# One more group gathered from the raw rows in a graph-network kernel, with its rows turned inside the group loop

## The chip, the cores and the metric

The kernel runs on one core of a Trainium2 chip. The metric is device time in microseconds, the median of several runs; lower is better. The engines are named as in the profile: PE (TensorE), DVE (VectorE), ACT (ScalarE), POOL (GpSimd) and SP (SyncE). SP, ACT and POOL also issue DMA transfers.

## The reference

There are 6250 nodes with 128 features and 100000 edges, sorted by destination, with 4 features each. All is float32.

```python
msg_in = concatenate([x[src], x[dst], edge_features], axis=1)
h = silu(msg_in @ mW1 + mb1)
messages = h @ mW2 + mb2
aggregated = segment_sum(messages, dst, num_segments=N)
u = silu(concatenate([x, aggregated], axis=1) @ uW1 + ub1)
updated = u @ uW2 + ub2
y = layer_norm(x + updated, ln_g, ln_b)
out = layernorm(x + y)
```

## The kernel before

**The algebra.** The first matrix `mW1` is split by its rows into a part for the source node, one for the destination node and one for the edge's features. Two tables of node rows are computed first: `tab_a = x @ (source part)` and `tab_b = x @ (destination part) + mb1`. Both are written to device memory. An edge's hidden row is then the row of `tab_a` at its source, plus a product which supplies the destination's and the edge features' share. Sums over destinations are made before the second matrix, so that `mW2` and the upper part of `uW1` can be merged into one matrix, `w2u` (`fuse_weights`).

**Groups.** Edges are worked in 98 groups of 1024, each of 8 tiles of 128 edges (the last has 6). For group g, `fetch(g)` (L273) has POOL issue one indirect DMA per tile, each of which gathers 128 rows of 512 bytes into the tile `ga`. There are 6 such buffers, in turn, so that group 6 takes the buffer of group 0 and so on. `products(g)` (L627) multiplies on PE a matrix `st` (which edge belongs to which of 96 nearby destinations, made by `node_matrix` on DVE, and the edge's features) with `mv` (96 rows of `tab_b` from the group's first destination, loaded by `load(g)` from SP, and the features' weights). `hidden(g)` (L640) adds the gathered rows on DVE and applies SiLU on ACT. `edge_matrix(g)` makes the one-hot `oh` on DVE, `by_nodes(g)` sums on PE the hidden rows by destination, and `add(g)` puts the sums into the accumulator `acc` on DVE.

**The first groups.** `tab_a` isn't written yet when the first gathers can start. So groups below `RAW`, here 5, gather rows of `x` itself. Those rows have to be multiplied by `w1`, and for that they are first turned by PE transposes: `turn_rows(g)` (L357) transposes the eight tiles of a group into a PSUM tile `wide` and has DVE copy them back over `rows[g]`. `products(g)` then adds one product of the turned rows per tile (L634), and `hidden(g)` has no addition on DVE. In the profile a float32 product counts as two MATMUL instructions, a transpose as one. The tables are computed in the loop of L367 beside all this; `turn_rows(0)` to `turn_rows(4)` are issued in it or just behind it, `products(0)` and `products(1)` follow at L685, before the loop of groups.

**The order of work** is written out by hand: the tile framework does not reorder the engines' instructions, each engine takes them in the order of the program. It still adds the waits that data need: a gather into a buffer that was used before waits for its last reader. Beside these, `fetch(g, a, b)` makes the first gather of a group wait for the PE instruction a and its fifth for b. The loop of groups (L688) runs at each g: the loads of group g + 4, `hidden(g)`, `products(g + 2)`, `node_matrix(g + 3)`, `edge_matrix(g + 1)`, `add(g - 2)`, `by_nodes(g)`, a `fetch`, and one step of each generator in `running`. Group 6 is fetched before the loop (L687), 7 at g = 0, 8 at g = 1, one group at every odd g up to 11, and from g = 12 on group g + 2.

**Side work as generators.** `destination_checks` (L230) tests whether all destinations of a group lie within 96 of its first, and whether finished nodes are really finished; if not, a general path runs at the end. It is begun at g = 2. `fuse_weights` (L450) is begun at g = 8. `node_batch` computes the output of four tiles of nodes at a time, first at g = 10. All three take their PSUM tile from `node_y` (L422), a pool with one buffer.

Of the kernel before, what the change touches and what calls it, by code (L numbers as in the profile page):

```python
# [24 lines left out]
def kernel(  # L25
# [40 lines left out]
    nc = tc.nc  # L66
# [5 lines left out]
    G = 8  # L72
# [6 lines left out]
    RB = 14  # L79
    CLOSE = 14  # L80
    LEAD = 4
    RAW = 5
    MADE = 3
    NQ = 4
    NM = 5
    BT = 4
# [28 lines left out]
    def wide():  # L115
        return tables_ps.tile([P, G, P], F32, name="wide")
# [51 lines left out]
    ident = consts.tile([P, P], F32, name="ident")  # L168
# [58 lines left out]
        nc.vector.tensor_copy(base_f, row)  # L227
        nc.vector.tensor_copy(base_i, row)

    def destination_checks(pm):  # L230

        nc.tensor.matmul(pm[:, 0, :NG], ones[0:1, :], base_f, start=True, stop=True)
        yield
        yield
        nc.vector.tensor_scalar(base_p, pm[:, 0, :NG], p_col, None, op0=OP.add)

        far = work.tile([P, 2], F32, name="far", bufs=1)
        nc.vector.tensor_reduce(far[:, 0:1], rel, AX.XY, OP.max)
        nc.vector.tensor_reduce(far[:, 1:2], rel, AX.XY, OP.min)
        mid = (W - 1) / 2  # L240
        nc.vector.tensor_scalar(far, far, -mid, None, op0=OP.add)
        nc.vector.tensor_mul(far, far, far)
        nc.vector.tensor_reduce(far[:, 0:1], far, AX.X, OP.max)
        farthest = work.tile([1, 1], F32, name="farthest", bufs=1)
        yield
        nc.tensor.transpose(pm[0:1, 1, :], far[:, 0:1], ident)
        yield
        yield
        nc.vector.tensor_reduce(farthest, pm[0:1, 1, :], AX.X, OP.max)
        bad = work.tile([1, 2], F32, name="bad", bufs=1)  # L250
        nc.vector.tensor_scalar(bad[:, 0:1], farthest, mid * mid, None, op0=OP.is_gt)

        below = work.tile([1, NG], F32, name="below", bufs=1)
        nc.vector.memset(below, 0.0)
        for i0, n, g in batches[:-1]:
            nc.vector.memset(below[:, g:], float((i0 + n) * P))
        nc.vector.tensor_sub(below, below, base_f)
        nc.vector.tensor_reduce(bad[:, 1:2], below, AX.X, OP.max)
        nc.vector.scalar_tensor_tensor(
            bad_i, bad[:, 1:2], 0.0, bad[:, 0:1], op0=OP.is_gt, op1=OP.max  # L260
        )
# [6 lines left out]
    rows, bases, near = {}, {}, {}  # L268

    def tiles_of(g):  # L270
        return min(G, -(-(E - g * GE) // P))

    def fetch(g, *after):  # L273

        rows[g] = gath.tile([P, G, H], F32, name="ga")
        for i in range(tiles_of(g)):
            ins = nc.gpsimd.indirect_dma_start(  # L277
                out=rows[g][:, i, :],
                out_offset=None,
                in_=x if g < RAW else tab_a[:, :],  # L280
                in_offset=bass.IndirectOffsetOnAxis(
                    ap=src_i[:, g, i : i + 1] if g else src_0[:, i : i + 1], axis=0
                ),
            )
            part, at = divmod(i * len(after), G)
            if after and at == 0 and after[part]:
                tc.add_manual_dep(
                    ins.ins,
                    after[part].ins.name,
                    mybir.DependencyInfo(  # L290
                        mybir.DependencyClass.Sync, mybir.DependencyReason.DATA
                    ),
                    reason="TensorE keeps up with the gathers",
                )
# [41 lines left out]
    def turn_x(i0, n):  # L336
        pt = wide()
        for i in range(n):
            ins = nc.tensor.transpose(pt[:, i, :], x_sb[:, i0 + i, :], ident)
        nc.scalar.copy(xT[:, i0 * P : (i0 + n) * P], pt[:, :n, :].rearrange("p i f -> p (i f)"))  # L340
        return ins
# [15 lines left out]
    def turn_rows(g):  # L357

        px = wide()
        for i in range(G):  # L360
            ins = nc.tensor.transpose(px[:, i, :], rows[g][:, i, :], ident)
        nc.vector.tensor_copy(rows[g], px)
        return ins

    turn_x(*parts[0])
    fetch(1)
    for k, (i0, n) in enumerate(parts):  # L367
# [5 lines left out]
        for j0, m in groups(n, G // 2):  # L373
            pm = wide().rearrange("p (i s) f -> p i s f", s=2)
# [24 lines left out]
        if k == 4:  # L399
# [1 line left out]
            destinations(0)  # L401
            load_bases(0)
            turn_rows(1)
    fetch(RAW, None, turn_rows(2))
    for g in range(3, RAW):
        turn_rows(g)
    if E < NG * GE:
        pad = tpool.tile([ED, NG * GE - E], F32, name="pad")
# [13 lines left out]
    def node_y():  # L422
        return node_ps.tile([P, BT, H], F32, name="y")
# [26 lines left out]
    def fuse_weights():  # L450
        pm = node_y()
        nc.tensor.transpose(pm[:, 0, :], raw_w["w2"], ident)
        yield
        w2T = work.tile([P, P], F32, name="w2T", bufs=1)
        nc.scalar.copy(w2T, pm[:, 0, :])
        yield
        nc.tensor.matmul(pm[:, 1, :], w2T, raw_w["u1a"], start=True, stop=True)
        nc.tensor.matmul(pm[0:1, 2, :], raw_w["mb2"], raw_w["u1a"], start=True, stop=True)
        yield
        nc.scalar.copy(w2u, pm[:, 1, :])  # L460
        nc.vector.memset(mb2u, 0.0)
        for k in range(DQ):
            nc.scalar.copy(mb2u[32 * k : 32 * k + 1], pm[0:1, 2, :])
# [150 lines left out]
    def edge_matrix(g):  # L614

        oh = work.tile([P, G, W], F32, name="oh", bufs=3)
        nc.vector.tensor_tensor(  # L617
            oh,
            w_row[:, None, :].to_broadcast([P, G, W]),
            rel[:, g, :, None].to_broadcast([P, G, W]),  # L620
            op=OP.is_equal,
        )
        return oh
# [3 lines left out]
    def products(g):  # L627
        pre = rows_ps()
        st = stbuf[g % NST].rearrange("k (i c) -> k i c", i=G)
        for i in range(tiles_of(g)):  # L630
            ins = nc.tensor.matmul(pre[:, i, :], st[:, i, :], mv[g % NM], start=True, stop=g >= RAW)  # L631
            begun.setdefault(g, ins)
            if g < RAW:
                ins = nc.tensor.matmul(  # L634
# [5 lines left out]
    def hidden(g):  # L640
        h = hbuf[g % NH]
        ga = rows.pop(g)
        n = tiles_of(g)
        s = pre.pop(g)
        if g >= RAW:
            ps = s
            s = work.tile([P, G, H], F32, name="s")
            nc.vector.tensor_add(s[:, :n], ga[:, :n], ps[:, :n])  # L648
        nc.scalar.activation(h[:, :n], s[:, :n], AF.Silu)  # L649
        return h  # L650
# [14 lines left out]
    def by_nodes(g, h, oh):  # L665

        pt = degrees(g)
        sums(g, pt, h, oh, 0, tiles_of(g))
        return pt
# [14 lines left out]
    oh, h, pt, running = {0: edge_matrix(0)}, {}, {}, []  # L684
# [3 lines left out]
    for g in range(NG):  # L688
        if g == 1:
            load_weights()  # L690
        if g == 2:
            running.append(destination_checks(node_y()))
        if g == 8:
            running.append(fuse_weights())
        for c in range(1, NC):
            if g == max(1, c * EC // GE - 10):
                attributes(c)
            if g == max(1, c * EC // GE - 10) + 1:
                attribute_rows(c)
        if g + LEAD < NG:  # L700
            load(g + LEAD)
        last = g >= NG - 1
        if not last:
            h[g] = hidden(g)
        if g + 2 < NG:
            pre[g + 2] = products(g + 2)
        if g + MADE < NG:
            node_matrix(g + MADE)
        if g + 1 < NG:
            oh[g + 1] = edge_matrix(g + 1)  # L710
        if g - 2 in pt:
            add(g - 2, pt.pop(g - 2))
        if last:
            break
        pt[g] = by_nodes(g, h.pop(g), oh.pop(g))
        if CLOSE <= g + 2 < NG:
            fetch(g + 2, begun[g + 2], summing[g])
        elif g == 0:
            fetch(7, ended[1], begun[2])
        elif g == 1:  # L720
            fetch(8, begun[3], summing[1])
        elif g % 2:
            fetch(g // 2 + 8, ended[g + 1], begun[g + 2] if g == CLOSE - 3 else ended[g + 2])
        if g >= NG - 3:
            add(g - 1, pt.pop(g - 1))
        for i0, n, first in batches[:-1]:
            if g == (first if first >= NG - 3 else first + 1):
                running.append(node_batch(i0, n, *node_tiles(nodes, node_y)))
        for _ in range(0 if g == NG - 2 else 4 if g == NG - 3 else 2 if g >= NG - 6 else 1):
            advance(running)  # L730
        if g == NG - 3:
            final = node_batch(
                *batches[-1][:2],
                nodes,

                lambda name, p=P: gath.tile([P, G, H], F32, name="ga")[:p, :BT],
                lambda: rows_ps()[:, :BT],
                final=True,
            )
            next(final)  # L740
        if g == NG - 2:
            next(final)

    g = NG - 1
# [25 lines left out]
    running = [before, final]  # L770
# [159 lines left out]
```

## Time and profile before

| what | value |
|---|---|
| median of 3 runs | 1169.08 us (1167.98 to 1169.18) |
| profiled execution | 1007.52 us |
| its span, first to last instruction | 1005.4 us |
| mean granted clock of PE | 0.739 |
| busy: PE, DVE, ACT, POOL | 682.9, 487.0, 238.9, 740.0 us |
| gathers by POOL from `tab_a` | 742, mean 944 ns |
| gathers by POOL from `x` | 32 for groups 1 to 4, 8 for group 0 |
| DMA | 89.01 MB, mean 89 GB/s |

The profile is of one execution; times in it count from its first instruction. In a line of a timeline the columns are start, duration, engine, line of the kernel, operation, tile written from tiles read, shapes and count; in brackets is the idle time of the engine before it and what ended it. A wait of one engine on several others is put down to the last of them. Busy POOL time is the time in which it prepares gathers; their data move later.

### The profile page before, as it was taken

The page shows a single profiled execution, that of the slowest core. Times are in us where ns is not written, and L with a number is a line of the kernel's source. Part 1 is how long each engine was busy: PE and PEld are TensorE (multiplying, and loading weights), DVE is VectorE, ACT ScalarE, POOL GpSimd, SP SyncE. Part 2 cuts the span into 40 slices and gives each one's busy share as a digit, 9 for nine tenths or more (in the row PEclk, how much of TensorE's full clock was granted, in tenths as well). Part 3 has the DMA queues.
Part 4 walks back from the last instruction along what each step waited for, and adds up shares of the span by engine and source line. Part 5 has one row for each costly group of instructions (what it writes and reads, how often), then busy time and mean ns, then how long its engine had stood idle before and what let it go on. Part 6 is the DMA issues. An engine that isn't in the chain of part 4 may idle for free. (4 is left out here: it accounts for less than half of the span.)

```text
span 1005.4 us, 11309 instructions
## 1 busy us (share of the span) xinstructions
PE 682.9 (68%) x3645; PEld 627.6 (62%) x3645; DVE 487.0 (48%) x1018; ACT 238.9 (24%) x295; POOL 740.0 (74%) x790
## 2 busy tenths in 40 slices
PE   5869766577676567757676756767757666766854
PEld 4759756567666566756665755766656666565752
DVE  5667625444544543643554453544453454264455
ACT  2312212220321131231222122122023113122233
POOL 7767777777777777777777777777777777777771
PEclk9979977777767677667667667667767775867776
DMA  9954332232323322333233224232332332322221
GB/s 229 266 159 115 98 76 58 75 93 77 85 75 83 85 76 57 86 83 97 54 96 87 68 63 113 60 93 65 88 84 75 83 75 76 83 59 76 66 76 29
DMA packets 70076, 89.01 MB, mean 89 GB/s; under 512 B 20703, under 2 KB 51694, under 8 KB 70010
## 3 DMA queue, kind: packets, MB, share of 16 engines
q0 software_dynamic: 25024, 51.30, 20.7%
q1 hardware_dynamic: 40408, 35.03, 12.4%
q10 hardware_dynamic: 4578, 1.89, 0.9%
q8 instruction: 31, 0.51, 0.2%
q14 instruction: 35, 0.29, 0.1%
HBM read 76.78 MB, written 11.38 MB: 88 GB/s over the span
## 5 line engine op out<-in xcount | busy, mean ns | idle before, releaser
L277 POOL DMA_INDIRECT ga<-tab_a,src_i x742 | 700.7, 944 | 231.1 <-issue 210.0
L631 PE MATMUL pre<-mv,st 100*128 100x128 f32 x1564 | 328.6, 390 | 282.1 <-DVE s L648 235.6
L631 PEld LDWEIGHTS pre<-mv,st 100*128 100x128 f32 x1564 | 300.5, 293 | 304.4 <-DVE s L648 255.5
L648 DVE TENSOR_TENSOR s<-ga,pre 128x1024 f32<-128x1024 f32 x92 | 112.3, 1221 | 460.1 <-DMA ga<-tab_a,src_i 459.5
L660 PE MATMUL pt<-oh,h 128*128 128x96 f32 x1564 | 254.0, 332 | 7.2 <-DVE deg L678 3.9
L660 PEld LDWEIGHTS pt<-oh,h 128*128 128x128 f32 x1564 | 252.9, 253 | 9.4 <-ACT acc_b L500 3.3
L649 ACT ACTIVATE h<-s 128x1024 f32<-128x1024 f32 x92 | 97.2, 1057 | 649.1 <-DVE s L648 649.1
L604 DVE TENSOR_SCALAR_CACHE_REDUCE st<-near,p_next 96x1024 f32<-96x1024 uint8 x98 | 124.2, 1269 | 2.2 <-issue 1.4
L617 DVE TENSOR_TENSOR oh<-w_row,rel 128x768 f32<-128x768 f32 x98 | 93.0, 949 | 11.5 <-PE pt L660 11.5
L277 POOL DMA_INDIRECT ga<-in_x_dram,src_i x32 | 30.3, 948 | 9.8 <-issue 8.8
L649 ACT ACT_TABLE_LOAD x23 | 29.5, 1283 | 26.0 <-DMA raw_mb<-in_L_gnn_mb_dram 19.6
L489 ACT ACT_TABLE_LOAD x24 | 30.8, 1283 | 7.9 <-DVE mv L484 7.5
L530 PEld LDWEIGHTS y<-u,uT 128*128 128x128 f32 x94 | 22.5, 323 | 8.9 <-issue 8.9
L530 PE MATMUL y<-u,uT 128*128 128x128 f32 x94 | 25.2, 415 | 0.0
L678 DVE TENSOR_TENSOR deg<-deg,pt 1x96 f32 x98 | 24.4, 249 | 1.0
L673 DVE TENSOR_TENSOR acc<-acc,pt 128x96 f32 x98 | 23.6, 241 | 0.1
L377 PE MATMUL wide<-w,xT 128*128 128x256 f32 x98 | 23.1, 391 | 0.2 <-DVE rel L200 0.2
L377 PEld LDWEIGHTS wide<-w,xT 128*128 128x128 f32 x98 | 18.9, 198 | 2.9 <-DVE rel L200 0.4
L484 DVE BATCH_NORM_AGGREGATE mv<-st 128x2 f32<-128x6 f32 x98 | 17.8, 182 | 3.4
L568 ACT ACTIVATE z<-z,shift,r 128x128 f32<-128x128 f32 x47 | 19.2, 479 | 0.3 <-DVE shift L562 0.3
L545 DVE SCALAR_TENSOR_TENSOR z<-y,r,xs 128x128 f32<-128x128 f32 x47 | 16.5, 351 | 1.7
L542 DVE SCALAR_TENSOR_TENSOR y<-y,mv,g_b 128x128 f32<-128x128 f32 x47 | 16.5, 351 | 1.3
(118 smaller groups left out, 327.5 us busy)
## 6 DMA issues: line engine op xcount, KB each, us to landing
ga<-tab_a,src_i POOLq DMA_INDIRECT x742, 2.6
near<-near_d SPq DMA_DIRECT2D x24, 384.0 KB
mv<-tab_b SPq DMA_DIRECT2D x98, 48.0 KB
tab_a<-t SPq DMA_DIRECT2D x6, 512.0 KB
tab_b<-x_sb SPq DMA_DIRECT2D x6, 512.0 KB
xs<-in_x_dram SPq DMA_DIRECT2D x11, 256.0 KB
out_dram<-z SPq DMA_DIRECT2D x11, 256.0 KB
st<-ea_d SPq DMA_DIRECT2D x98, 16.0 KB
```

The lines of the kernel that those rows point to most:

```text
L277: ins = nc.gpsimd.indirect_dma_start(out=rows[g][:, i, :], out_offset=None, in_=x if g < RAW else tab_a[:, :], in_offset=bass.IndirectOffs ...
L377: ins = nc.tensor.matmul(pm[:, j], xT[:, cols], w1, start=True, stop=True)
L489: nc.scalar.activation(r[:, :n], mv[:, :n, 1], AF.Sqrt, bias=eps)
L530: nc.tensor.matmul(y[:, i, :], by_p[:, :, i], u2, start=final, stop=final or i == n - 1)
L604: nc.vector.tensor_scalar(stbuf[g % NST][:W], near.pop(g), p_next, 0.0, op0=OP.is_equal, op1=OP.add, accum_out=deg_q[g // DQ % 2][:, g % D ...
L617: nc.vector.tensor_tensor(oh, w_row[:, None, :].to_broadcast([P, G, W]), rel[:, g, :, None].to_broadcast([P, G, W]), op=OP.is_equal,)
L631: ins = nc.tensor.matmul(pre[:, i, :], st[:, i, :], mv[g % NM], start=True, stop=g >= RAW)
L648: nc.vector.tensor_add(s[:, :n], ga[:, :n], ps[:, :n])
L649: nc.scalar.activation(h[:, :n], s[:, :n], AF.Silu)
L660: ins = nc.tensor.matmul(pt[:, :W], h[:, i, :], oh[:, i, :], start=i == 0, stop=i == tiles_of(g) - 1)
L673: nc.vector.tensor_add(at, at, pt[:, :W])
L678: nc.vector.tensor_add(at, at, pt[row, W:])
```

## The change

`RAW` becomes 6, so group 5 is gathered from `x` and gets the second product in `products(5)`. Its rows aren't turned in front of the loop: a generator `turn_late` does it in two halves of four tiles, through the PSUM tile of `node_y`, with steps at g = 1, 2 and 3, between `hidden(g)` and `products(g + 2)`. `fuse_weights` begins at g = 4 instead of 8 and `destination_checks` at g = 7 instead of 2; the latter takes its PSUM tile at its first step and has two empty steps fewer.

```diff
-    RAW = 5
+    RAW = 6
...
-    def destination_checks(pm):
-
+    def destination_checks():
+
+        pm = node_y()
         nc.tensor.matmul(pm[:, 0, :NG], ones[0:1, :], base_f, start=True, stop=True)
-        yield
         yield
         nc.vector.tensor_scalar(base_p, pm[:, 0, :NG], p_col, None, op0=OP.add)
...
         nc.tensor.transpose(pm[0:1, 1, :], far[:, 0:1], ident)
-        yield
         yield
         nc.vector.tensor_reduce(farthest, pm[0:1, 1, :], AX.X, OP.max)
...
+    def turn_late(g):
+
+        for lo in range(0, G, BT):
+            px = node_y()
+            for i in range(BT):
+                nc.tensor.transpose(px[:, i, :], rows[g][:, lo + i, :], ident)
+            yield
+            nc.vector.tensor_copy(rows[g][:, lo : lo + BT], px)
...
-    fetch(RAW, None, turn_rows(2))
-    for g in range(3, RAW):
+    fetch(RAW - 1, None, turn_rows(2))
+    for g in range(3, RAW - 1):
         turn_rows(g)
...
-        if g == 2:
-            running.append(destination_checks(node_y()))
-        if g == 8:
+        if g == 4:
             running.append(fuse_weights())
+        if g == 7:
+            running.append(destination_checks())
...
             h[g] = hidden(g)
+        if g == 1:
+            late = turn_late(RAW - 1)
+        if 1 <= g <= 3:
+            next(late, None)
         if g + 2 < NG:
             pre[g + 2] = products(g + 2)
```

## The prediction

> **What bounds the kernel now.** I read the busy shares, the gatherer's waits, and then each engine's timeline between 50 and 100 us. The page and the groups come first (the gather groups: busy us, mean ns of one, then idle us before them):
>
> ```profile
> POOL 7767777777777777777777777777777777777771
> L277 POOL DMA_INDIRECT ga<-tab_a,src_i x742 | 700.7, 944 | 231.1 <-issue 210.0
> L277 POOL DMA_INDIRECT ga<-in_x_dram,src_i x32 | 30.3, 948 | 9.8 <-issue 8.8
> ```
>
> POOL works evenly through the span. 742 + 32 + 8 (group 0) = 782 gathers, each 0.944 us plus 0.30 us of issue: 782 x 1.247 = 975 us of 1005.4. The last gather ends at 985.1; the other 20.3 us are its landing and the closing of the last nodes, which the chain of waits shows and which the change doesn't touch. So a microsecond is won only where POOL waits longer than 0.30 us. POOL's waits list two such places beside its very first gather (total us, times, longest us):
>
> ```profile
> POOL ga L277 <- DMA tab_a<-t: 4.1, 1, 4.1
> POOL ga L277 <- PE pre L634: 1.5, 1, 1.5
> ```
>
> On POOL's timeline (start, duration, wait before it), the last gather of group 4, the first and last of group 5, and the first of group 6:
>
> ```profile
> 52.37 0.94 POOL L277 DMA_INDIRECT ga<-in_x_dram,src_i  x1 [0.30 <-issue]
> 57.37 0.94 POOL L277 DMA_INDIRECT ga<-tab_a,src_i  x1 [4.06 <-DMA tab_a<-t]
> ...
> 66.11 0.94 POOL L277 DMA_INDIRECT ga<-tab_a,src_i  x1 [0.30 <-issue]
> 68.56 0.94 POOL L277 DMA_INDIRECT ga<-tab_a,src_i  x1 [1.51 <-PE pre L634]
> ```
>
> The avoidable stalls are 4.06 - 0.30 = 3.76 us (group 5 waits for the table) and 1.51 - 0.30 = 1.21 us (group 6 reuses the buffer of group 0, which `products(0)` on PE still reads). The question is what sets the second. The timeline of all engines from 56 us, then PE's:
>
> ```profile
> 56.44 0.18 PEld L361 LDWEIGHTS wide<-ident,ga 128*128 128x128 f32 x1 [0.27 <-DMA ga<-in_x_dram,src_i]
> 56.95 1.23 DVE L362 COPY ga<-wide 128x1024 f32<-128x1024 f32 x1 [2.98 <-PE wide L361]
> ...
> 58.19 0.35 DVE L409 MEMSET pad<- 4x352 f32 x1
> ...
> 58.57 0.31 SPq L410 DMA_DIRECT2D ea_d<-pad  x1
> ...
> 59.20 0.36 SPq L599 DMA_DIRECT2D mv<-tab_b  x1
> ...
> 62.53 0.76 PE L631 MATMUL pre<-mv,st 100*128 100x128 f32 x2 [5.62 <-DMA mv<-tab_b]
> ```
> ```profile
> 67.90 0.39 PE L634 MATMUL pre<-w,ga 128*128 128x128 f32 x2
> ```
>
> The reader is to follow one chain: group 4's last rows land (56.44), PE turns them, DVE copies them back (to 58.17), clears `pad`, SP sends `pad` (58.57) and only then loads `mv` (59.20), which lands at 62.5; `products(0)` runs 62.53 to about 68.1, and POOL goes on at 68.56 after its own 0.30 us. Nothing in this chain is group 5's gather. It hangs on group **4**, whose gathers end at 53.31 in either kernel.
>
> **What the Trainium skill says.** "DMA: Bandwidth & Descriptors", section "SWDGE vs HWDGE vs iDMA": the DMA engines round-robin between queues fed by GpSimd and by SP, so earlier gathers share the engines with table writes. The trace agrees that there is something to share: in 53 to 54 us the engines are full (323 GB/s), in 57 to 59 empty. "TensorE: Matmul & The Clock Gate", section "Part 1: The HAM clock gate": the gate opens after some 3.4 us of activity, in a free-running window, so the moment varies by run. Here 0.50 was granted from 57 to 66 us and 1.0 afterwards; the variation no run here shows. The same page's first table: VectorE and ScalarE take instructions in strict order; the trace agrees: before the one-hot compare at 77.34 us DVE stood 6.53 us, waiting for PE, and did nothing else. "SBUF — State Buffer", section "SBUF: two separate sides": a VectorE operation in a two-port mode keeps GpSimd from writing descriptors. One gather took 1.10 us at 37.23, beside VectorE's conversions of destinations; of 782 gathers only five exceed 1.0 us, and the change adds copies out of PSUM, which have no such visible effect at 56.95.
>
> **The change, part by part.**
>
> *Group 5 from x.* `tab_a` is no longer waited for at 53.6: group 5 starts at 53.31 + 0.30 = 53.61, 3.76 us earlier, ends its issue at 67.05 - 3.76 = 63.29. Removed: -3.76. Its fifth gather also waits for `turn_rows(2)`, on PE by about 51.4, against 58.6: nothing.
>
> *Where the stall goes.* Group 6 still waits for `products(0)`, released at 68.26: its excess becomes 68.26 - 63.29 = 4.97 instead of 1.21. Added: +3.76. Sum 0. The new wait on `tab_a` at group 6 is hidden behind it (the table was there at 57.07). If the chain on group 4 were shorter, the cover would go: all 4.97 us could be won.
>
> *DMA crowding.* Of group 5, two gathers (64 KB each by rows of 512 bytes) now reach the engines before these drain at 56: 128 KB / 310 GB/s = 0.4 us that the table writes or group 4's landing may be late. Not visible before; bounds: 0 (the writes of `tab_b` alone are late, with 59.2 - 56.4 = 2.8 us to spare before `mv` is loaded) and 0.8 us (four gathers ahead of group 4's last rows). I take 0.2.
>
> *Turning group 5 in the loop.* 8 transposes, 1.04 us for 8 in the row of L361, half in g = 1, half in g = 2; two DVE copies, half of 1.22 us each plus overhead, 0.69 by the 128x512 additions of L380. PE runs without a gap from 62.5 to 105 us, so PE work here is real. The eight extra pairs in `products(5)`: with rows of x 3.60 us start to start (77.14 to 80.74), without 1.89 (88.34 to 90.23): +1.71. The checks' first matmul leaves this stretch: -0.39. So `products(5)` ends at 90.4 + 1.0 + 1.7 - 0.4 = 92.7, and later groups on PE about 2.3 to 3 us late, with the fused weights' 0.27 + 0.42 + 0.38 us at g = 4 and 6. Who waits: gathers of group 8 need the start of `products(3)` (77.14, now 77.6; slack before 11.4), of group 9 the ends of `products(4)` and `products(5)` (slack 12.5 and 13.1), of group 10 those of 6 and 7 (14.5 and 15.8). I got the slack as POOL's start less PE's event. 3 out of 12: hidden, cost 0.
>
> *In-order waits added.* DVE's first copy waits for PE until 77.6; behind it stand the node matrix of group 5 (was at 69.53, now 78.4 to 79.7), and the one-hot of 3. Their users run at about 89 and 92. PE's second half waits for DVE's first copy: done at 78.4, needed at 83. `products(5)` at 89 waits for the second copy, about 84.3. Rows of group 5 have landed by about 67, ten us before PE reads them. All hidden. `hidden(5)` loses its DVE addition (1.22 us), ScalarE reads PSUM instead.
>
> *Moved checks and fusing.* The checks' first DVE part, 2.66 us (89.10 to 91.75), goes to g = 8, the second, 3.2 us (103.16 to 106.38), to g = 10. DVE waits for gathers there: 1.28 us before the addition at 111.43, 5.63 before 129.91; and the 3.2 us gone from g = 7 bring g = 8 forward. Hidden; if not, POOL's slack of 13 us at group 13 takes it. Fusing moves from g = 8..11 to 4..7: five ScalarE copies of 0.25 us and a memset of 0.17, beside ScalarE waits of 3 to 6 us. Its raw weights are issued by 66.7 and read after 90. The two leave the single y buffer in turn: turning ends at g = 3, fusing at 7, checks at 10, the first node batch asks for it at 11. No DMA is added or removed; SP's queue keeps its order; on POOL only the table of eight gathers changes.
>
> Sum: -3.76 + 3.76 + 0.2 = +0.2 on the profiled execution of 1007.52 (span 1005.4, 2.1 around it). The runs' median, 1169.08, lies 161.6 above that execution, and no view says why; I carry that over whole. If it is instead a stretch of everything by 1.16, the zero stays zero and 0.2 hardly grows.
>
> **Rivals.** A change of 0.2%, 2.3 us, is about what a measurement of this kernel can tell from none.
>
> *The stall is really won (faster).* For: POOL bounds the kernel and 4.97 us are idle. Against: the release at 68.26 hangs on group 4. Warm PE from the start would take `products(0)` from 5.5 to 3.6 us, and POOL would be released at 66.3 instead of 68.26: before it would then start at 67.35, after at 66.6, 0.8 us won. For 2.3 us the chain has to be about 3.6 us shorter, or `tab_a` later by that against group 4's landing. Full gain 4.97: 1164.1.
>
> *PE's backlog reaches POOL (slower).* Place: gathers of groups 9 and 10. If the gate stays at half in 66 to 110 us, products take 6.9 (with x rows) and 3.7 us, sums 3.6 (3.74 and 3.53 are seen at 121 and 125 us): `products(4)` then ends at 104 against POOL's need at 100. From there every microsecond that PE gets more is POOL's: transposes 2.0 + products 3.4 = +5.4 us, 1174.5. It decides once the backlog eats the slack of 12.5 us. Against: 1.0 was granted throughout in this stretch.
>
> *Crowding (slower).* 0.8 us is my bound; to pass 2.3 us, 310 GB/s x 2.3 = 0.7 MB would have to stand ahead, more than the group's 0.5 MB, or a late `tab_b` would have to push `mv`. 1172.
>
> **How the numbers follow.** Moved stall, no net change: 0.72. Won: 0.13. Backlog: 0.10. Crowding over 0.2%: 0.05. So faster 0.13, same 0.72, slower 0.15. The likeliest time is 1169.08 + 0.2 = 1169.3. Range 1166 to 1171.8: it holds the likeliest case with its -0.8 to +0.8 and the spread of the runs, half of the gains, and most of the crowding; the full gain and the backlog, under 0.2 together, stay out.
>
> **What would show it.** Right: 40 gathers from x and 734 from the table, no wait before group 5, one wait of about 5.3 us before the first gather of group 6, ended by `products(0)` near 68.3, and the last gather within 1 us of 985. Wrong: group 6 starting near 64 to 66 (won), any new wait of POOL above 0.3 us at groups 8 to 13 (backlog), or `products(0)` starting later than 63 (crowding).

## The result and the profile after

The changed kernel takes 1174.26 us (median of 20 runs, 1170.67 to 1178.53) against 1171.07 us for the kernel before (20 runs): a ratio of 1.0027, with a 95% interval of 1.0017 to 1.0038. It is slower by some 3.2 us, outside the range that was forecast.

The executions on record are of two kinds, and in every later job, a set of kernels run together, all were of one kind: on the fast kind the kernel before takes 1007.5 to 1009.1 us, on the slow kind, to which the timed pair belongs, 1162 to 1171 us (three executions far off their job, at 1184.65, 1210.96 and 2185.05 us, are in no ratio). The expectations on record call these two kinds of chip. That it is the chip is not shown: the chips of the later jobs are numbered, and numbers 10 and 12 stand under both kinds. The first profile of the kernel before, on which the prediction rests, came from the fast kind. The profile of the changed kernel came from the slow kind: its execution took 1171.88 us and its span 1169.8 us.

So the two profiles can't be set side by side as they stand. The page of the changed kernel, and the groups of its gathers (busy us, mean ns of one, idle us before them):

```profile
POOL 6655666666666566666665666566666666665661
L276 POOL DMA_INDIRECT ga<-tab_a,src_i x734 | 695.3, 947 | 380.1 <-issue 198.5
L276 POOL DMA_INDIRECT ga<-in_x_dram,src_i x40 | 38.1, 952 | 20.4 <-issue 11.0
```

The counts are those of the change, 734 and 40, and a gather still costs 0.947 us. But the idle time before the 734 is 380.1 us, of which 0.30 us each explain 220. In the chain of waits that ended last, 20% of the span is PE's and 13% is time in which nothing is waited for. POOL's waits (total us, times, longest us):

```profile
POOL ga L276 <- remote: 128.0, 43, 3.6
POOL ga L276 <- PE pre L639: 29.3, 18, 4.9
POOL ga L276 <- PE pre L642: 10.1, 2, 8.7
```

The waits called "remote" are ended by an event that the profile can't put down to an instruction. 33 of the 43 stand from group 16 on, at the first gather of an even group, mostly 16 gathers apart, and last 2.6 to 3.6 us; `fetch` makes these gathers wait for PE. The rows around groups 5 and 6 answer to those of the prediction; POOL's timeline first, then the timeline of all engines:

```profile
70.97 0.94 POOL L276 DMA_INDIRECT ga<-in_x_dram,src_i  x1 [0.30 <-issue]
80.59 0.94 POOL L276 DMA_INDIRECT ga<-tab_a,src_i  x1 [8.68 <-PE pre L642]
```
```profile
64.82 0.53 PE L360 MATMUL wide<-ident,ga 128*128 128x128 f32 x2 [0.84 <-issue]
...
66.98 3.48 DVE L361 COPY ga<-wide 128x1024 f32<-128x1024 f32 x3 [3.03 <-remote]
70.48 0.35 DVE L417 MEMSET pad<- 4x352 f32 x1
...
71.50 0.35 SPq L607 DMA_DIRECT2D mv<-tab_b  x1
...
74.84 0.77 PE L639 MATMUL pre<-mv,st 100*128 100x128 f32 x2 [9.49 <-DMA st<-ea_d]
```

The wait for the table is gone and a wait for `products(0)` stands at group 6, as forecast. But DVE begins to copy groups 2 to 4 back only at 66.98, after 3.03 us for which no instruction answers. The kernel before on the slow kind, with which that is to be compared, stands further down.

### The profile page after: what moved, and what is told of

Its sections match the earlier page's. It is cut to its first block, busy times and chain, and to the rows that moved or that the text cites. A ratio compares the mean times of both kernels' runs of the same rounds, so it can differ in the third digit from the quotient of the medians.

```text
span 1169.8 us, 11354 instructions
## 1 busy us (share of the span) xinstructions
PE 732.9 (63%) x3669; PEld 667.2 (57%) x3669; DVE 486.7 (42%) x1019; ACT 238.0 (20%) x295; POOL 742.6 (63%) x790
## 5 line engine op out<-in xcount | busy, mean ns | idle before, releaser
L276 POOL DMA_INDIRECT ga<-tab_a,src_i x734 | 695.3, 947 | 380.1 <-issue 198.5
L639 PE MATMUL pre<-mv,st 100*128 100x128 f32 x1564 | 339.6, 389 | 226.5 <-issue 200.1
L639 PEld LDWEIGHTS pre<-mv,st 100*128 100x128 f32 x1564 | 309.4, 295 | 247.4 <-issue 231.3
L668 PE MATMUL pt<-oh,h 128*128 128x96 f32 x1564 | 291.6, 346 | 159.6 <-issue 159.3
L668 PEld LDWEIGHTS pt<-oh,h 128*128 128x128 f32 x1564 | 280.4, 265 | 174.2 <-issue 173.8
L276 POOL DMA_INDIRECT ga<-in_x_dram,src_i x40 | 38.1, 952 | 20.4 <-issue 11.0
L540 DVE TENSOR_TENSOR y<-y,xs 128x512 f32<-128x512 f32 (+1 forms) x12 | 8.3, 688 | 75.4 <-issue 75.4
L526 ACT ACTIVATE uT<-y,ub_col 128x512 f32<-128x512 f32 (+1 forms) x12 | 8.1, 678 | 101.8 <-remote 69.3
L642 PE MATMUL pre<-w,ga 128*128 128x128 f32 x96 | 20.8, 301 | 0.0
```

The lines of the kernel that those rows point to most:

```text
L276: ins = nc.gpsimd.indirect_dma_start(out=rows[g][:, i, :], out_offset=None, in_=x if g < RAW else tab_a[:, :], in_offset=bass.IndirectOffs ...
L668: ins = nc.tensor.matmul(pt[:, :W], h[:, i, :], oh[:, i, :], start=i == 0, stop=i == tiles_of(g) - 1)
```

## The experiments

Ratios are against the kernel before, unchanged, run beside each in the same job. Theory A: PE's added work in groups 1 to 5 makes a backlog that reaches POOL. Theory B: the moved checks and merging cost the time. Theory C, which became G: gathering group 5 early costs it, because `products(0)` starts later. The first four runs take the change apart.

**The kernel before, as it is.**

> The kernel before, unchanged, timed against itself and profiled once more. All theories: ratio 1.000 within 0.001. Its span is expected near 1168 us as in the timed runs, not 1005 us as in the first profile, and its POOL timeline should show stalls of about 3.4 us every 16 gathers, as the changed kernel's does. Theory A (PE's backlog reaches POOL): POOL waits for PE at groups 8 to 14 here too, but by about 3 us less in sum than the 17 us of the changed kernel, and group 6 still waits for products(0).

It fell on the fast kind: 1007.83 us, ratio 0.9995 (0.9987 to 1.0003), so nothing of the stalls was to be seen. It does give the noise of a single profile: `products(0)` starts at 62.9 us here, 62.5 in the first profile, and group 6 at 69.2 and 68.6.

**The moves alone.** `RAW` stays 5, nothing is turned late; the checks are those of the change:

```diff
-        if g == 2:
-            running.append(destination_checks(node_y()))
-        if g == 8:
+        if g == 4:
             running.append(fuse_weights())
+        if g == 7:
+            running.append(destination_checks())
```

> Only the checks and the merging of weights moved (checks begin at g = 7, merging at g = 4); five groups from x as before. Theory A (PE's added work in groups 1 to 5 is the cost): same as before, ratio 0.999 to 1.001. Theory B (the moved side work is the cost): 1.0027, 3 us slower. Theory C (gathering group 5 early is the cost): 1.000.

Fast kind: 0.9996 (0.9987 to 1.0004).

**The early gather alone.**

```diff
-                in_=x if g < RAW else tab_a[:, :],
+                in_=x if g < RAW + 1 else tab_a[:, :],
```

> Only group 5's gathers read x instead of the table; its rows are neither turned nor multiplied by w1, so group 5's messages leave that product out. Nothing moved. Theory A: 1.000, the wait for the table goes and comes back at group 6. Theory B: 1.000. Theory C (early gathers crowd the DMA engines and products(0) starts later): 1.0027, with group 6 starting 3 us later than in the unchanged kernel.

Fast kind: 0.9995 (0.9987 to 1.0003). In the profile group 5 starts at 54.0 instead of 58.0 us, and group 6 at 68.9 instead of 69.2.

**PE's work and the moves, without the early gather.** In the changed kernel:

```diff
-                in_=x if g < RAW else tab_a[:, :],
+                in_=x if g < RAW - 1 else tab_a[:, :],
```

> The changed kernel, but group 5 is gathered from the table again; its rows are still turned and multiplied by w1, so group 5's messages have that product twice over. All of PE's added work and the moves are there, the early gather isn't. Theory A: 1.0027, as slow as the changed kernel. Theory B: 1.0027 as well (with moves 1.0027). Theory C: 1.000.

Fast kind: 1.0000 (0.9992 to 1.0008). All four say nothing of the slow kind, but they agree with the prediction's sum for the kind of which its profile was. The whole change was run there as well.

> The changed kernel, unchanged. The four runs before it came from a chip on which the kernel before takes 1007.5 us and POOL stalls nowhere but at groups 5 and 6, unlike the timed pair of 1171 and 1174 us. On a chip of that kind theory A, as the parts suggest (0.9995 to 1.000 each), expects 1.000 within 0.001: group 6 starts near 68.5 us, the same as before, and PE's backlog is below POOL's slack of 11 to 13 us. On a chip of the other kind (the kernel before near 1171 us) it expects 1.0027 again. Theories B and C expect 1.003 on either.

1008.17 us against 1008.49, ratio 1.0001 (0.9990 to 1.0011). POOL's only excess wait behind its first gathers:

```profile
POOL ga L276 <- PE pre L642: 6.3, 1, 6.3
```

That is the moved stall of the prediction: nothing at group 5 (started at 53.7 us), all of it at group 6 (69.7).

**A backlog made by hand.** To see what PE's added work is worth when PE is late, both kernels got 14 more products in each `by_nodes` of groups 0 to 12:

```diff
         pt = degrees(g)
+        for _ in range(14 if g <= 12 else 0):
+            nc.tensor.matmul(pt[:, :W], h[:, 0, :], oh[:, 0, :], start=True, stop=True)
         sums(g, pt, h, oh, 0, tiles_of(g))
```

> The kernel before with PE slowed by hand in groups 0 to 12: the first product of every by_nodes is made 14 times more (3.2 us of PE per group, overwritten afterwards, so the result stays). This makes PE late on a chip on which it isn't. Two PE groups per POOL group then need about 14 us against POOL's 10, so the slack of 12 us at group 9 is gone by group 10. Theory A (PE's backlog reaches POOL) expects waits for PE of some 10 to 25 us in sum at groups 10 to 14, and the kernel longer by that.

> The changed kernel with the same slowing. Theory A: once PE's backlog reaches POOL, the change's added PE work (1.0 us of transposes, 1.7 us of products, less 0.4 us of checks moved away) passes on whole: 2 to 3 us more than slow_before, where the unslowed pair differed by nothing (1.0001). Rival D (the slow chip's difference is something else, such as where its stalls fall in a longer instruction stream): no difference between the slowed pair on a chip of the fast kind.

Fast kind: 1.0143 (1.0124 to 1.0162) and 1.0155 (1.0138 to 1.0171). POOL waited for PE at groups 10 or 11 to 14, as expected. From the start of `products(0)` to that of `products(9)` PE needed 62.3 us without the change and 64.8 with it, 2.5 us more. The medians, 1022.74 and 1023.37 us, differ by less, and not clearly. In this pair of profiles `products(0)` also started 3.2 us earlier with the change (61.4 against 64.6 us). A further profile of the kernel before fell on the fast kind (1007.62 us). It widens the noise of a single profile: `products(0)` starts at 61.9 us and group 5 at 55.5, where the two before it have 57.4 and 58.0.

> The kernel before, unchanged, once more, for a profile on a chip of the slow kind if the run falls on one (the kernel before near 1171 us). There theory A expects the same stalls of all engines as in the changed kernel's profile, waits of POOL for PE at groups 8 to 14 that are about 3 us shorter in sum than the changed kernel's 17 us, and one wait for products(0) at group 6. On a chip of the fast kind: 1007.5 us and nothing new.

**A dose of PE work,** with and without the slowing, and the slowed pair again:

```diff
     for i in range(tiles_of(g)):
+            for _ in range(4 if g == RAW - 1 else 0):
+                nc.tensor.matmul(pre[:, i, :], st[:, i, :], mv[g % NM], start=True, stop=True)
             ins = nc.tensor.matmul(pre[:, i, :], st[:, i, :], mv[g % NM], start=True, stop=g >= RAW)
```

> The changed kernel with more of its own kind of work: every first product of group 5 is made four times more (32 float32 products, 64 MATMUL instructions, some 7 us of PE; overwritten, so the result stays). No other slowing. Theory A: products(5) ends near 93.3 + 7 = 100.4 us in the profile, still before POOL needs it at about 104.6 (fifth gather of group 9), so nothing: 0.999 to 1.001 of the kernel before. Rival D (PE's instructions cost time by their number alone): + 7 us or part of it.

> slow_after with the same 7 us of PE work in products(5). Theory A: PE is behind POOL from group 10 on, so all 7 us show: 1.007 above slow_after, about 1030 us. Against A: the same as slow_after, 1023 us.

> slow_before again, for more runs of the pair: 1.0143 of the kernel before, as it was.

> slow_after again. Theory A, corrected by the first pair's profiles: products(0) to products(9) took 62.3 us there without the change and 64.8 with it, so 2.5 us more of PE, but the first pair's medians differ by 0.6 us only. If A is right the pair differs by 1 to 2.5 us over both jobs; if the early gather lets products(0) start sooner (theory F: 61.4 us against 64.6 in that one pair of profiles), the two cancel and the difference stays near 0.5.

All on the fast kind. Without slowing, the 7 us more cost nothing: 1.0002 (0.9994 to 1.0011). With it they show in full: 1.0241 (1.0225 to 1.0257) against 1.0171 (1.0156 to 1.0187) for the slowed changed kernel beside it, 0.0070 or 7.1 us of 1009. The pair itself came out at 1.0151 (1.0133 to 1.0170) and 1.0171, so over both jobs the change costs 0.0012 and 0.0020 when PE is behind: in the right direction and of the size of theory A's lower bound, but in neither job clear of the intervals. In the second pair of profiles PE needed 63.2 and 64.7 us, only 1.5 us more with the change. This shows a rule (PE's work is free until its backlog eats POOL's slack, and then costs its length). It does not show that the rule was at work in the measured pair.

**The slow kind.**

> The kernel before, for its profile on a chip of the slow kind, if this run falls on one (1171 us). Theory A: all engines stall as in the changed kernel's profile there, and POOL's waits for PE at groups 8 to 14 are about 3 us shorter in sum than the 17 us seen there. Against A: those waits are as long, and the 3 us lie elsewhere. On a chip of the fast kind: 1007.5 us.

> The changed kernel with group 5 gathered from the table (its product with w1 twice over), beside it. On a chip of the slow kind theory A expects 1.0027, as the changed kernel; theory C (the early gather is the cost) 1.000. On one of the fast kind 1.000 again.

Both fell on it: 1164.82 us for the kernel before (1163.02 over 27 runs). With PE's work and the moves, but without the early gather, it takes 1162.64 us: 0.9991 (0.9983 to 0.9999). Theory A expected 1.0027 here, and so did B. **Both fall.** POOL's waits at groups 8 to 14, beyond 0.30 us each, come to 14.6 us here, against 17.1 in the first profile of the changed kernel. That is the sign which theory A asked for, but it compares two jobs: in the profile of the whole change below they come to 14.6 us as well, and from the start of group 6 to that of group 14 both kernels take 94.4 us. The timeline of the kernel before on the slow kind:

```profile
63.02 3.42 DVE L362 COPY ga<-wide 128x1024 f32<-128x1024 f32 x3
63.65 0.62 PE L361 MATMUL wide<-ident,ga 128*128 128x128 f32 x2 [0.52 <-DMA ga<-in_x_dram,src_i]
...
66.83 0.31 SPq L410 DMA_DIRECT2D ea_d<-pad  x1
67.46 0.36 SPq L599 DMA_DIRECT2D mv<-tab_b  x1
67.94 0.94 POOL L277 DMA_INDIRECT ga<-tab_a,src_i  x1 [8.31 <-DMA tab_a<-t]
...
70.57 0.77 PE L631 MATMUL pre<-mv,st 100*128 100x128 f32 x2 [6.30 <-DMA st<-ea_d]
...
79.70 0.94 POOL L277 DMA_INDIRECT ga<-tab_a,src_i  x1 [2.08 <-remote]
```

Here POOL stands still from 59.6 to 67.9 us, because the table comes 8.31 us late for it, and in that silence DVE copies three groups back without a break. `products(0)` starts at 70.57, where the changed kernel's single profile had 74.84.

**The early gather alone, and the whole change, on the slow kind.**

> Only group 5's gathers read x (its messages leave out the product with w1), nothing else changed. On a chip of the slow kind peonly_2 gave 0.9991, which contradicts theories A and B there: PE's work and the moves aren't the cost. Theory G: on such a chip all engines freeze after some number of gathers; POOL going on through 60 to 65 us brings a freeze into the turning of group 4, DVE's copies start at about 67 instead of 63 us, and products(0) at about 74.8 instead of 70.6. It expects 1.0027 there, with products(0) at 74 to 75 us. Against G: 1.000 or less, products(0) near 70.6 us. On a chip of the fast kind: 1.000.

> The changed kernel beside it. On a chip of the slow kind all theories expect 1.0027 again, as in the measured pair; theory G expects it no slower than xgather_2 within 0.001, since the rest of the change costs nothing there. On one of the fast kind: 1.000, as after_again.

1167.30 us, ratio 1.0042 (1.0028 to 1.0055), for the early gather alone; 1167.77 us, 1.0041 (1.0028 to 1.0055), for the whole change. So the early gather alone makes the loss. Theory G had the place right and the size too small (1.0027, `products(0)` at 74 to 75 us). The timeline of the early gather alone:

```profile
63.94 0.64 PE L361 MATMUL wide<-ident,ga 128*128 128x128 f32 x2 [0.75 <-issue]
...
65.53 1.23 DVE L362 COPY ga<-wide 128x1024 f32<-128x1024 f32 x1 [2.36 <-issue]
...
69.52 0.95 POOL L277 DMA_INDIRECT ga<-in_x_dram,src_i  x1 [0.30 <-issue]
72.58 2.35 DVE L362 COPY ga<-wide 128x1024 f32<-128x1024 f32 x2 [5.83 <-remote]
...
75.95 0.36 SPq L599 DMA_DIRECT2D mv<-tab_b  x1
...
79.09 0.77 PE L631 MATMUL pre<-mv,st 100*128 100x128 f32 x2 [14.51 <-DMA st<-ea_d]
```

PE's last transposes of group 4 start at the same time in both (63.65 and 63.94 us for the last row of two): group 4 has not landed later. But DVE stands 2.36 and 5.83 us before its copies, in which this timeline names no instruction that it waits for. It goes on at 72.58, 2.1 us after POOL's last gather of the group has ended (69.52 + 0.95). In the whole change in this job it is the same: POOL's last gather ends at 69.55, and then come:

```profile
71.94 2.36 DVE L361 COPY ga<-wide 128x1024 f32<-128x1024 f32 x2 [7.30 <-remote]
...
78.45 0.76 PE L639 MATMUL pre<-mv,st 100*128 100x128 f32 x2 [13.88 <-DMA mv<-tab_b]
...
85.35 0.94 POOL L276 DMA_INDIRECT ga<-tab_a,src_i  x1 [15.79 <-PE pre L642]
```

In the first profile after, POOL paused from 65.26 to 67.22 us, and there DVE went on at 66.98.

The trace also holds the semaphore events, and they say what the timeline doesn't. A semaphore is the counter by which one engine tells another that it is done; DVE's copies wait for the one that PE counts up with each transpose (and for those of the gathers' landings, which PE has waited for before). In the kernel before its events come every 0.11 us, from 60.85 to 63.14, and end at 64.28 us. In the early gather alone single ones stand at 64.09, 66.89, 68.29 and 69.72 us, and more from 71.12 on, the last at 72.83, 8 us after PE's own rows have ended (64.58). DVE goes on among these last ones. So by these events what comes late is PE's signal, and not its work. They are not complete, though: a profile of the slow kind holds 4563 to 4731 semaphore events, one of the fast kind some 18000.

The DMA engines do not explain it, as the windows show (busy us and count of PE, weight loads, DVE, ACT and POOL, then granted clock, share of the DMA engines, GB/s). The kernel before on the slow kind:

```profile
66.00:68.00 2.00, 0.00 (x0) 0.00 (x0) 0.95 (x3) 0.00 (x0) 0.06 (x1) 0.61 0.40 115
68.00:70.00 2.00, 0.00 (x0) 0.00 (x0) 1.66 (x3) 0.00 (x0) 1.70 (x2) 0.50 0.26 71
70.00:72.00 2.00, 1.43 (x7) 1.46 (x8) 2.00 (x5) 0.00 (x0) 1.39 (x3) 0.50 0.46 134
```

and the early gather alone:

```profile
66.00:68.00 2.00, 0.00 (x0) 0.00 (x0) 0.75 (x1) 0.00 (x0) 1.66 (x2) 0.50 0.98 284
68.00:70.00 2.00, 0.00 (x0) 0.00 (x0) 0.00 (x0) 0.00 (x0) 1.43 (x2) 0.50 0.23 66
70.00:72.00 2.00, 0.00 (x0) 0.00 (x0) 0.00 (x0) 0.00 (x0) 0.47 (x1) 0.50 0.17 53
```

The tables' writing does end about 1 us later (the engines are full up to 68 us). But from 68 to 72 us they are at 0.17 to 0.23, POOL alone works, up to 70.47, and everything else stands.

**POOL held.** If POOL's gathering at that time is the cause, and not the reading of `x`, a hold undoes the loss. POOL is held at group 5 until DVE has copied group 4 back (in `turn_rows` the copy's instruction is kept in `copied`):

```diff
-    fetch(RAW - 1, None, turn_rows(2))
-    for g in range(3, RAW - 1):
+    for g in range(2, RAW - 1):
         turn_rows(g)
+    fetch(RAW - 1, copied[-1])
```

> xgather (group 5's gathers read x, its messages leave out the product with w1), but POOL is held at the first of them until DVE has copied group 4's turned rows back. Theory G (on the slow kind of chip, gathers that go on back to back keep DVE and PE from going on, so group 4 is turned late): there 1.000 within 0.0012, against 1.0042 for xgather_2, with products(0) back at 70 to 71 us and DVE's copies at 63 to 66.5. Against G (it is reading x, not the time at which it is read): 1.004. On a chip of the fast kind 1.000, as everything.

> The whole change with the same hold. Theory G: on the slow kind of chip 0.999 to 1.001, as peonly_2 (0.9991); against G 1.004. On the fast kind 1.000.

Slow kind again: 1160.96 us, 0.9983 (0.9973 to 0.9992), for the early gather with the hold; 1161.64 us, 0.9983 (0.9974 to 0.9992), for the whole change with it. So the hold undoes the loss, and the time at which group 5 is gathered is the cause. Both ratios lie even below those forecast, 1.6 and 0.9 us by the medians; where such a gain would come from is not shown, and the run of PE's work and the moves, which takes nothing away, came out at 0.9991 too. The timeline of the whole change, held:

```profile
63.20 3.42 DVE L361 COPY ga<-wide 128x1024 f32<-128x1024 f32 x3
```
```profile
66.89 0.95 POOL L276 DMA_INDIRECT ga<-in_x_dram,src_i  x1 [6.46 <-DVE ga L361]
...
78.66 0.94 POOL L276 DMA_INDIRECT ga<-tab_a,src_i  x1 [2.06 <-PE pre L642]
```

DVE's three copies run at 63.2 without a break, group 5 starts at 66.9 instead of 67.9, and group 6 at 78.7 instead of 79.7 (85.3 in the unheld change). In the early gather held they run at 64.5 and `products(0)` starts at 72.0, 1 us later than forecast. Group 14 starts at 173.3, in the early gather held at 174.1, against 174.1 in the kernel before and 179.8 in the change: the 5.7 us lost in front of the loop stay lost, none are made up. From group 14 to group 97 the three kernels take the same, 953.3 to 954.3 us.

## Why the prediction was wrong

**The step that failed** is the end of the working, "I carry that over whole. If it is instead a stretch of everything by 1.16, the zero stays zero". The 161.6 us between the profiled execution and the runs were neither an addend nor an even stretch. The slow kind behaves otherwise: from group 14 to group 97 POOL needs 954 us there instead of 830, through stalls that no row of the first profile shows. The sum was right for the kind of its profile (1.0001 measured for +0.2 us) and was applied to one where group 5's gather does bear on its chain: the sum had put 0.2 us on that, and `products(0)` starts 7.9 us later. Of the 5.0 us by which 1174.26 misses 1169.3, the change is 3.2; the other 2.0 are its base, 1169.08 in three runs and 1171.07 in twenty.

**Group 5 from x, -3.76.** Right in kind. On the fast kind group 5 starts 1.8 to 4.3 us earlier (55.5 to 58.0 in three profiles before, 53.7 after). On the slow kind it is 8.0 us (67.9 to 59.9), since the table is later there, so there was more to move.

**Where the stall goes, +3.76 at group 6.** Right: 6.25 us wait on the fast kind (5.3 forecast; `products(0)` started 1.3 us later in that profile than in the first), with no net change. On the slow kind the wait at group 6 is 15.8 us, because what releases it became later itself.

**DMA crowding, 0.2 us with bounds of 0 and 0.8.** This is the term that was mis-sized. On the slow kind `products(0)` starts 7.9 us later (70.57 to 78.45), group 6 starts 5.6 us later (79.7 to 85.3), and 5.3 us of it come through to the end (1167.77 less 1162.45; 4.8 by the ratio); in the measured pair it was 3.2. Its mechanism was wrong as well: I looked for late data, but group 4's rows are turned at the same time, and the late step is DVE's copy, which by the semaphore events PE's signal reaches late, while from 68 us on the DMA engines are three quarters idle. "Nothing in this chain is group 5's gather" held for what waits for what, and not for when it is told. The sign by which crowding was to be told, `products(0)` starting late, was the right one to watch; the reason beside it wasn't.

**PE's work in the loop and the in-order waits, 0.** Right on both kinds: 1.0000 and 0.9991 with all of it and no early gather. The size was about right: 2.5 and 1.5 us more of PE in the two slowed pairs, against "2.3 to 3 us".

**Moved checks and fusing, 0.** Right: 0.9996 alone on the fast kind, and contained in the 0.9991 on the slow.

**The rivals.** The backlog was a good description of a threshold, as the dose of 7 us shows (0.2 us without a backlog, 7.1 with one), but not of what happened: it was given 0.10, and crowding, whose place was right, 0.05. That its 1174.5 lies beside the measured 1174.26 is chance. (Its "need at 100" should read 98.5, where group 9's first gather stands before.) The gain that was given 0.13 was not there.

**What stays open.** Why PE's signal comes late while POOL gathers is not shown; the load of the DMA engines doesn't explain it. What makes an execution slow isn't shown either. A rival that no run tests is the recording itself: on the slow kind three quarters of the semaphore events are missing from every profile, and each timed execution has its span and clock from such records too. The hold was measured on the slow kind alone.

## What to carry to other kernels

When the profiled execution and the timed runs differ by more than noise, the profile describes another situation than the one that is timed: a sum that comes to zero in it has no sign elsewhere, and its range must say so. A stall of the engine that bounds the kernel can be shelter for others; before it is removed, look at what runs in that silence and whether it is on the chain that ends the next stall. If so, the freed engine can be made to wait for just that work, as the hold does here.

## What the runs showed of the hardware

On the slow kind PE gets on slowly while POOL issues gathers one after another, and no wait that the profile shows explains it. In the profile of the changed kernel 16 MATMULs of the first `by_nodes`, 1.9 us of work on the fast kind, took from 87.9 to 103.6 us, while POOL issued gathers at 1.25 us. The kernel before has the same there: its PE timeline shows products one or two at a time:

```profile
92.58 0.60 PE L634 MATMUL pre<-w,ga 128*128 128x128 f32 x2 [1.03 <-issue]
93.98 0.37 PE L631 MATMUL pre<-mv,st 100*128 100x128 f32 x1 [0.80 <-issue]
95.39 0.57 PE L631 MATMUL pre<-mv,st 100*128 100x128 f32 x1 [1.04 <-issue]
```

POOL then stops for some 3 us every 16 gathers, and PE catches up: in the profile of the changed kernel POOL stood from 197.60 to 200.82 us, and from 200.44 on PE did 12 MATMULs in 2.87 us. The kernel before on the slow kind has 40 such stops after group 14, of 3.1 to 3.5 us, and all 40 stand where `fetch` makes POOL wait for PE: PE, slow beside the gathers, makes POOL wait in its turn. That gives 1.439 us per gather over 80 groups (921 us for 640 gathers from group 17 to 97) instead of 1.25. A gather itself costs the same on both kinds, 0.944 and 0.947 us. So on the slow kind about 3 us of every 23 are lost in this way, far more than the change could move.
